# Two of four scans per unit take a constant start and carry the state in an extra column

## The chip, the cores and the metric

The kernel runs on one core of one Trainium2 chip. The metric is device microseconds of one execution. The kernel before takes 7170.91 us (median of 3 runs, 7170.88 to 7171.45). Its profile is of one further execution.

## The reference, cut to what matters

Two layers work on x of shape (4, 128, 128, 128), all in float32. The first is a Mamba block over L = 16384 positions per image with 256 inner channels and 16 states per channel, followed by a group norm, silu and a residual. The second layer mixes spectra of each channel with four filters (rfft2 and irfft2 as matrix products). The change touches only the recurrence of the first layer:

```python
def step(h, inp):
    d_t, B_t, C_t, u_t = inp
    dA = jnp.exp(d_t[:, :, None] * A)
    h = h * dA + d_t[:, :, None] * B_t[:, None, :] * u_t[:, :, None]
    y = jnp.einsum('bds,bs->bd', h, C_t)
    return (h, y)
```

`h` starts at zero for each image, and is carried over all 16384 positions.

## The kernel before, in words

`block0` is the first layer, `block1` the second. In `block0` time is cut into **chunks** of T = 512 positions, 32 to an image (`NCH`), 128 in all. Within a chunk the 256 channels times 16 states are 32 tiles of 128 partitions by 512 positions (32 channels by 4 states each). Four such tiles form a **unit**: half `j` of the channels (2), rotation `r` (4), so a chunk has 8 units, here u0 to u7 in order, and u6 is (j, r) = (1, 2). The four tiles of a unit are its **places** 0 to 3.

For each place the work is: ScalarE computes exp(delta*A) into a tile `da` (L393, "exp 0" to "exp 3" below); VectorE runs `tensor_tensor_scan` (L412, "scan 0" to "scan 3"), which computes state = da*state + du*B along the 512 positions, starting from the last state of the same tile of the chunk before (`last`, a [P, 2] tile `st`), or from the constant 0.0 where an image begins; the states are multiplied with C into `hb`; and TensorE sums `hb` over the states into `y` (L433). The products with C are GpSimd's for places 0 and 1 (L419, one instruction for both, the scans having written to an SBUF tile `h`) and VectorE's for places 2 and 3 (L414, the scans having written in place over `da`). `by_vector` (L347) makes exceptions: in odd chunks that are not "norming", place 1 of u6 is VectorE's too. In **norming** chunks (16 of 32 in each of the later three images, 48 of 128, in which the image before is normalised beside the scans) place 2 of u6 is GpSimd's.

du*B comes from two places. For places 1 to 3 GpSimd multiplies it into `hb` (L363). For place 0 TensorE turns it into PSUM (`dbu_turn`, L383, four transposes, "the turn", tile `b0`). `b0` and `da` of places 1, 2 and 3 are PSUM tiles of one bank each, with one buffer each; `da` of place 0 lies in SBUF with two buffers.

The order on every engine is written out by hand: each chunk has 16 slots, two per unit (even slot: places 0 and 1, odd slot: places 2 and 3), and each slot goes through the phases of L552 in order. Each engine's queue is what that walk emits. Dependencies between engines are semaphore waits that the tile framework inserts; PSUM accesses to one bank are ordered by bank. The parts that matter here:

- ScalarE, in the odd slot of unit u: exp 1 of unit u+1 (phase "exps"); the copy of the last states of places 0 and 1 (`st<-h`, phase "late", L420, shown as L554); the chunk's other work ("act", "pool"); exp 0 of unit u+2 ("early"); the two copies of the last states of places 2 and 3 (`st<-da`, L415). In the next even slot: exp 2 and exp 3 of unit u+1, then other work.
- TensorE, in the odd slot of unit u: the turn of unit u+1 first, then sums of unit u-1, then the chunk's other matmuls.
- GpSimd: `dbu` of unit u+1, then the product with C of unit u.

The other work of ScalarE for the next chunk sits in fixed slots (L323 to L332): silu and z in slot 2 (u1), softplus in slot 6 (u3), the turned copies `bt` in slots 8 to 14, of which those of slots 8 and 11 wait for transposes `pt_dut` of TensorE that precede them directly. From chunk 52 on, transforms of the second layer are mixed in (`spectrum`, slots 12 and 13, L468).

Of the kernel before, what the change touches and what calls it, by code (L numbers as in the profile page):

```python
# [26 lines left out]
F32 = mybir.dt.float32  # L27
AF = mybir.ActivationFunctionType
ALU = mybir.AluOpType
# [4 lines left out]
P = 128  # L34
T = 512
DG = 32
SQ = 4
NP = 16
# [8 lines left out]
def kernel(ctx: ExitStack, tc: tile.TileContext, a: dict, out: bass.AP):  # L47
# [101 lines left out]
    spec = [dpool.tile([H, C, 2, WF], F32, tag=f"spec_{b}", name=f"spec_{b}") for b in range(EARLY)]  # L149
    shared = SimpleNamespace(**{k: v for k, v in locals().items() if k not in ("ctx", "tc")})  # L150
    block0(tc, shared)
    block1(tc, shared)


def block0(tc, s):
    nc, B, NCH, NH, NS, NG, ND, R, NX, KC, HALO, C, L, NF, DI = (
        s.nc, s.B, s.NCH, s.NH, s.NS, s.NG, s.ND, s.R, s.NX, s.KC, s.HALO, s.C, s.L, s.NF, s.DI,
    )
    NT = T // P
    with ExitStack() as ctx:  # L160
        def pool(name, bufs, **kw):
            return ctx.enter_context(tc.tile_pool(name=name, bufs=bufs, **kw))

        p1 = pool("p1", 1)
        p2 = pool("p2", 2)
        hpool = pool("hb", 4)
        tiny = pool("tiny", 2)
# [5 lines left out]
        psd = pool("psd", 1, space=PSUM)  # L173
# [4 lines left out]
        def turn_bank(n):  # L178
            return pst.tile([P, T], F32, tag="pt", name=f"pt_{n}")

        st = {}
        stats, outs = s.stats, s.outs

# [154 lines left out]
        def norming(k):  # L338

            return k >= NCH and 2 <= k % NCH < 2 + NCH // 2  # L340

        def place(r, p):


            return (p - r) % ND

        def by_vector(k, j, r, p):  # L347

            if norming(k):
                return p > 1 and (j, r, p) != (1, 2, 2)  # L350
            return p > 1 or (k % 2 == 1 and (j, r, p) == (1, 2, 1))

        def dbu(u):

            k, r = divmod(u, NH * NG)
            j, r = divmod(r, NG)
            d = st[k]
            hb = d["hb", j, r] = hpool.tile([P, ND, T], F32, tag="hb", name=f"hb_{k}_{j}_{r}")
            p = 1
            while p < NG:  # L360
                m = place(r, p)
                n = min(NG - p, ND - m)
                nc.gpsimd.tensor_tensor(  # L363
                    hb[:, p : p + n, :], d["du", j][:, m : m + n, :], d["B"][:, p - 1 : p - 1 + n, :], ALU.mult
                )
                p += n

        def pair(n):

            k, r = divmod(n, NP)  # L370
            u, p = divmod(r, ND // 2)
            j, r = divmod(u, NG)
            return k, j, r, 2 * p

        def dbu_turn(n):

            k, j, r, p = pair(n)
            d = st[k]
            if p == 0:
                b = d["b0"] = psd.tile([P, T], F32, tag="b0", name=f"b0_{k}_{j}_{r}")  # L380
                for t in range(NT):
                    src = d["bt"][:, t, j * ND + place(r, 0), :, :].rearrange("p s d -> p (s d)")
                    nc.tensor.transpose(b[:, t * P : (t + 1) * P], src, s.ident)  # L383

        def exps(n, qs):

            k, j, r, p = pair(n)
            d = st[k]
            for q in qs:
                m = place(r, p + q)  # L390
                c = (j * NG + p + q) * ND + m
                da = (psd if p + q else p2).tile([P, T], F32, tag=f"da{p + q}", name=f"da{p + q}_{k}_{j}_{r}")
                nc.scalar.activation(da, d["delta", j][:, m, :], AF.Exp, scale=s.amat[:, c : c + 1])  # L393
                d["da", j, r, p + q] = da

        def scans(n):


            k, j, r, p = pair(n)
            d = st[k]  # L400
            hb = d["hb", j, r]
            das = [d.pop(("da", j, r, p + q)) for q in range(2)]
            dve = [q for q in range(2) if by_vector(k, j, r, p + q)]
            pool = [q for q in range(2) if q not in dve]
            last = d["last", j, r, p] = tiny.tile([P, 2], F32, tag=f"st{j}_{r}_{p}", name=f"st_{k}_{j}_{r}_{p}")
            if pool:
                h = p2.tile([P, 2, T], F32, tag="h", name=f"h_{k}_{j}_{r}_{p}", bufs=3)
            for q in range(2):
                b = hb[:, p + q, :] if p + q else d.pop("b0")
                init = 0.0 if k % NCH == 0 else st[k - 1]["last", j, r, p][:, q : q + 1]  # L410
                o = das[q] if q in dve else h[:, q, :]
                nc.vector.tensor_tensor_scan(o, das[q], b, init, ALU.mult, ALU.add)  # L412
            for q in dve:
                nc.vector.tensor_tensor(hb[:, p + q, :], das[q], d["C"][:, p + q, :], ALU.mult)  # L414
                nc.scalar.copy(last[:, q : q + 1], das[q][:, T - 1 : T])  # L415
            if pool:
                q = slice(pool[0], pool[-1] + 1)
                ps = slice(p + pool[0], p + pool[-1] + 1)
                nc.gpsimd.tensor_tensor(hb[:, ps, :], h[:, q, :], d["C"][:, ps, :], ALU.mult)  # L419
                todo[n + 1, "late"].append(partial(nc.scalar.copy, last[:, q], h[:, q, T - 1]))  # L420

        def sums(u):

            k, r = divmod(u, NH * NG)
            j, r = divmod(r, NG)
            d = st[k]
            if r == 0:
                y = d["y", j] = psy.tile([P, T], F32, tag="y", name=f"y_{k}_{j}")
                nc.tensor.matmul(y, s.diag[:, j, :], d["u"][:, j, :], start=True, stop=False)  # L429
            y = d["y", j]  # L430
            for p in range(ND):
                m = place(r, p)
                nc.tensor.matmul(  # L433
                    y[m * DG : (m + 1) * DG, :], s.sel, d["hb", j, r][:, p, :], start=False, stop=r == NG - 1
                )

        def post(k):
# [66 lines left out]
        n_chunks = B * NCH  # L504
        todo = defaultdict(list)
# [33 lines left out]
        for n in range(n_chunks * NP):  # L539
            if n % 2 == 0:  # L540
                todo[n - 3, "early"].append(partial(exps, n, (0,)))
            todo[n - 1, "exps"].append(partial(exps, n, (1,) if n % 2 == 0 else (0, 1)))
            todo[n - 1, "turn"].append(partial(dbu_turn, n))
            todo[n, "scans"].append(partial(scans, n))
            if n % 2 == 0:
                todo[n - 2, "dbu"].append(partial(dbu, n // 2))
            else:
                todo[n + 2, "sums"].append(partial(sums, n // 2))
        slots = [n for n, _ in todo]
        with tc.manual_schedule():  # L550
            for n in range(min(slots), max(slots) + 1):
                for phase in ("turn", "sums", "pe", "exps", "late", "act", "pool", "dbu", "early", "gate", "scans", "dve", "end"):  # L552
                    for f in todo[n, phase]:
                        f()  # L554

# [500 lines left out]
```

## Time and profile before

| what | value |
|---|---|
| median of 3 runs | 7170.91 us |
| the profiled execution | 7175.45 us, of which the span from first to last instruction is 7173.6 us |
| VectorE busy in the span | 6892.9 us (96%) |
| GpSimd busy | 6892.5 us (96%) |
| ScalarE busy | 6143.9 us (86%) |
| TensorE busy | 5904.2 us (82%), mean granted clock 0.897 |
| scans (L412) | 4096 of about 1.2 us |
| `block0` | from the start to about 6408 us; the rest is `block1` |

The busy shares are averages over stages. In `block0` a chunk takes 48.37 us (even) or 49.12 us (odd) where nothing else is mixed in, and 50.30 us where norming is. In the groups of instructions each row has a line, an engine, an operation, the tiles out<-in, and then busy time, mean nanoseconds of one and the idle time before it with what ended it. In the timeline each row has start, duration, engine, line and operation, and in brackets the engine's idle time before it and what ended it; on VectorE and ScalarE the next instruction starts some 0.08 us before the one before it ends, so what an instruction costs its engine is the distance of starts.

### The profile page before, as it was taken

What the parts mean: (1) busy time and instruction counts of PE and PEld (TensorE: products, weight loads), DVE (VectorE), ACT (ScalarE), POOL (GpSimd) and SP (SyncE); (2) the same over time, 40 slices, a digit from 0 to 9 for tenths busy, and PEclk for the clock granted to TensorE, in tenths of its full rate; (3) what the DMA queues carried; (4) which work ended last, traced back from release to release, by engine and by line L of the source; (5) the groups of instructions that cost most, each with busy time, mean ns of one, the idle gap of its engine ahead of it and who ended that gap; (6) DMA issues with size and microseconds to landing.
All of it is one profiled execution on the core that took longest, in us unless ns stands there. A gap on an engine that the chain in (4) does not pass through costs nothing.

```text
span 7173.6 us, 91384 instructions
## 1 busy us (share of the span) xinstructions
PE 5904.2 (82%) x26708; PEld 2626.8 (37%) x26708; DVE 6892.9 (96%) x7966; ACT 6143.9 (86%) x13658; POOL 6892.5 (96%) x3188
## 2 busy tenths in 40 slices
PE   6888888788787788888888788888887888867998
PEld 2333333233222233333333333333333333326888
DVE  6999999999999999999999999999999999989777
ACT  6888888888888888888888888898888888878876
POOL 6999999999999999999999999999999999988887
PEclk8888888888888889998989899999898899979999
DMA  5666666666777777777777777777777777769866
GB/s 139 160 160 152 163 159 151 165 159 165 191 176 192 179 171 176 172 184 175 189 196 186 188 176 175 178 177 184 189 191 194 177 179 177 172 164 306 236 185 162
DMA packets 905480, 1286.20 MB, mean 179 GB/s; under 512 B 81672, under 2 KB 356752, under 8 KB 904976
## 3 DMA queue, kind: packets, MB, share of 16 engines
q1 hardware_dynamic: 904832, 1280.09, 71.9%
q8 instruction: 210, 3.44, 0.2%
q14 instruction: 294, 2.41, 0.1%
q10 hardware_dynamic: 144, 0.26, 0.0%
HBM read 1023.45 MB, written 256.58 MB: 178 GB/s over the span
## 4 chain that ended last, share of the span: by engine, by line
DVE 41%; ACT 29%; issue 11%; PE 10%; DMA 5%; POOL 3%; SPq 1%; DVEq 0%; ACTq 0%; POOLq 0%
DVE da L412 20%; DVE h L412 12%; ACT da L393 12%; DVE hb L414 5%; ACT L393 3%; DMA rdelta<-dd 2%; ACT L275 2%; ACT delta L275 2%; ACT bt L304 2%; POOL hb L363 2%; DVE zs L443 1%; PE y L433 1%; POOL hb L419 1%; ACT L242 1%; DMA xt<-x 1%
## 5 line engine op out<-in xcount | busy, mean ns | idle before, releaser
L363 POOL TENSOR_TENSOR hb<-rdu,rB 128x1536 f32<-128x1536 f32 (+2 forms) x1536 | 3605.7, 2364 | 22.4 <-DMA rdelta<-dd 21.3
L393 ACT ACTIVATE da<-rdelta,amat 128x512 f32<-128x512 f32 x4096 | 2794.1, 700 | 138.3 <-DVE h L412 133.9
L419 POOL TENSOR_TENSOR hb<-h,rC 128x1024 f32<-128x1024 f32 (+1 forms) x1072 | 2435.0, 2274 | 88.8 <-DVE h L412 73.4
L412 DVE TENSOR_TENSOR_SCAN da<-da,st,hb 128x512 f32<-128x512 f32 x1976 | 2419.8, 1267 | 21.5 <-ACT da L393 14.3
L433 PE MATMUL y<-hb,sel 128*32 128x512 f32 x8192 | 1313.4, 717 | 2.9 <-POOL hb L419 2.7
L414 DVE TENSOR_TENSOR hb<-da,rC 128x512 f32<-128x512 f32 x2040 | 1296.1, 674 | 3.0
L412 DVE TENSOR_TENSOR_SCAN h<-da,st,b 128x512 f32<-128x512 f32 x992 | 1258.3, 1268 | 1.7 <-PE b L383 1.6
L412 DVE TENSOR_TENSOR_SCAN h<-da,st,hb 128x512 f32<-128x512 f32 x1000 | 1251.6, 1255 | 1.8 <-ACT da L393 1.8
L383 PE MATMUL b<-ident,bt 128*128 128x128 f32 x4096 | 748.4, 305 | 516.1 <-DVE h L412 390.6
L234 PE MATMUL pp_cv<-xm,wck 128*128 128x512 f32 x2048 | 1014.3, 640 | 1.6 <-ACT xm L217 0.8
L304 ACT ACTIVATE bt<-pt_dut,xdt 128x256 f32<-128x256 f32 x2048 | 839.4, 474 | 184.5 <-PE pt_dut L293 184.3
L383 PEld LDWEIGHTS b<-ident,bt 128*128 128x128 f32 x4096 | 531.3, 154 | 1017.1 <-DVE h L412 692.8
L415 ACT COPY st<-da 128x1 f32<-128x1 f32 x2040 | 273.1, 160 | 474.2 <-DVE hb L414 471.1
L234 PEld LDWEIGHTS pp_cv<-xm,wck 128*128 128x128 f32 x2048 | 395.9, 204 | 651.0 <-issue 422.1
L828 POOL TENSOR_TENSOR wb<-wb,term 128x1040 f32<-128x1040 f32 x192 | 461.0, 2401 | 70.8 <-ACT term L822 62.9
L293 PE MATMUL pt_dut<-ident,du 128*128 128x128 f32 x1024 | 232.4, 338 | 285.1 <-ACT xdt L286 174.9
L429 PE MATMUL y<-u,diag 128*128 128x512 f32 x512 | 303.0, 675 | 188.7 <-DVE zs L443 187.3
L293 PEld LDWEIGHTS pt_dut<-ident,du 128*128 128x128 f32 x1024 | 132.2, 162 | 604.8 <-POOL du L312 475.9
L393 ACT ACT_TABLE_LOAD x262 | 336.1, 1283 | 12.1 <-DMA rdelta<-dd 7.4
L312 POOL TENSOR_TENSOR du<-delta,u 128x512 f32<-128x512 f32 x256 | 318.8, 1267 | 25.8 <-ACT delta L275 25.8
L223 PE MATMUL pp_z<-xm,win 128*128 128x512 f32 x512 | 274.5, 634 | 51.8 <-ACT fq L497 46.2
L267 PE MATMUL pp_dt<-xd,wdt 8*128 8x512 f32 x512 | 284.8, 642 | 33.0 <-ACT pp_o L457 23.5
(160 smaller groups left out, 8139.8 us busy)
## 6 DMA issues: line engine op xcount, KB each, us to landing
rdelta<-dd SPq DMA_DIRECT2D x1024, 256.0 KB, 4.7
rdu<-dd SPq DMA_DIRECT2D x1024, 256.0 KB, 7.5
rC<-bc SPq DMA_DIRECT2D x512, 256.0 KB, 7.3
rB<-bc SPq DMA_DIRECT2D x512, 192.0 KB, 4.7
dd<-delta SPq DMA_DIRECT2D x256, 256.0 KB, 7.2
dd<-du SPq DMA_DIRECT2D x256, 256.0 KB, 5.7
ft<-in_filt_w SPq DMA_DIRECT2D x104, 520.0 KB, 7.0
ob<-o SPq DMA_DIRECT2D x128, 256.0 KB, 2.1
```

Source lines behind the costliest of these rows:

```text
L234: nc.tensor.matmul(ps["cv", j], w, d["xm"][:, t : t + T], start=t == 0, stop=t == KC - 1)
L293: nc.tensor.transpose(ps["dut"][:, 2 * t + j, :], d["du"][:, j, at : at + P], s.ident)
L304: nc.scalar.activation(d["bt"][:, 2 * h + t, :, q, :], src, AF.Copy, scale=d["xdt"][:, 2 * h + t, R + q : R + q + 1])
L312: nc.gpsimd.tensor_tensor(du, d["delta"][:, j, :], d["u"][:, j, :], ALU.mult)
L363: nc.gpsimd.tensor_tensor(hb[:, p : p + n, :], d["du", j][:, m : m + n, :], d["B"][:, p - 1 : p - 1 + n, :], ALU.mult)
L383: nc.tensor.transpose(b[:, t * P : (t + 1) * P], src, s.ident)
L393: nc.scalar.activation(da, d["delta", j][:, m, :], AF.Exp, scale=s.amat[:, c : c + 1])
L412: nc.vector.tensor_tensor_scan(o, das[q], b, init, ALU.mult, ALU.add)
L414: nc.vector.tensor_tensor(hb[:, p + q, :], das[q], d["C"][:, p + q, :], ALU.mult)
L419: nc.gpsimd.tensor_tensor(hb[:, ps, :], h[:, q, :], d["C"][:, ps, :], ALU.mult)
L433: nc.tensor.matmul(y[m * DG : (m + 1) * DG, :], s.sel, d["hb", j, r][:, p, :], start=False, stop=r == NG - 1)
L828: nc.gpsimd.tensor_tensor(wb, wb, u[n].terms[f], ALU.add)
```

## The change

The scans of places 1 and 2 become 513 columns long and start from the constant 0.0. Their first column holds the last state of the chunk before: `hb` gets one more column in front (`1 + T`), into which a new small ScalarE copy (`carry`, phase "carry" in the odd slot before the unit, after "late") writes the two states; at an image's start GpSimd clears it instead. The first column's factor does not matter, since it multiplies the constant 0.0: it is whatever lies in PSUM just before `da`. For that, `b0` and `da` of places 1 and 2 become one tile `band` of three banks, and the scan of place 1 reads from the last column of `b0` on, that of place 2 from the last column of `da` of place 1 on. The scan of place 2 also writes that column when it runs in place.

Since the scan of place 2 now touches the bank of place 1, exp 1 of the next unit is issued after the scans of the odd slot, no longer at the slot's start. `last` becomes one [P, 4] tile per unit. `by_vector` gives place 1 of u6 to VectorE in even chunks too (outside norming ones); that unit (in which the scans of places 1 and 2 keep their pointer to the state) is the one that `carried` leaves out.

```diff
--- before.py
+++ after.py
@@ -178,6 +178,7 @@
         def turn_bank(n):
             return pst.tile([P, T], F32, tag="pt", name=f"pt_{n}")
 
+        band = psd.tile([P, 3 * T], F32, tag="band", name="band")
         st = {}
         stats, outs = s.stats, s.outs
 
@@ -348,22 +349,37 @@
 
             if norming(k):
                 return p > 1 and (j, r, p) != (1, 2, 2)
-            return p > 1 or (k % 2 == 1 and (j, r, p) == (1, 2, 1))
+            return p > 1 or (j, r, p) == (1, 2, 1)
 
         def dbu(u):
 
             k, r = divmod(u, NH * NG)
             j, r = divmod(r, NG)
             d = st[k]
-            hb = d["hb", j, r] = hpool.tile([P, ND, T], F32, tag="hb", name=f"hb_{k}_{j}_{r}")
+            hb = d["hb", j, r] = hpool.tile([P, ND, 1 + T], F32, tag="hb", name=f"hb_{k}_{j}_{r}")
             p = 1
             while p < NG:
                 m = place(r, p)
                 n = min(NG - p, ND - m)
                 nc.gpsimd.tensor_tensor(
-                    hb[:, p : p + n, :], d["du", j][:, m : m + n, :], d["B"][:, p - 1 : p - 1 + n, :], ALU.mult
+                    hb[:, p : p + n, 1:], d["du", j][:, m : m + n, :], d["B"][:, p - 1 : p - 1 + n, :], ALU.mult
                 )
                 p += n
+
+        def carried(k, j, r):
+
+            return () if by_vector(k, j, r, 1) else (1, 2)
+
+        def carry(u):
+
+            k, r = divmod(u, NH * NG)
+            j, r = divmod(r, NG)
+            if carried(k, j, r):
+                o = st[k]["hb", j, r][:, 1:3, 0]
+                if k % NCH == 0:
+                    nc.gpsimd.memset(o, 0.0)
+                else:
+                    nc.scalar.copy(o, st[k - 1]["last", j, r][:, 1:3])
 
         def pair(n):
 
@@ -377,7 +393,7 @@
             k, j, r, p = pair(n)
             d = st[k]
             if p == 0:
-                b = d["b0"] = psd.tile([P, T], F32, tag="b0", name=f"b0_{k}_{j}_{r}")
+                b = band[:, 0:T]
                 for t in range(NT):
                     src = d["bt"][:, t, j * ND + place(r, 0), :, :].rearrange("p s d -> p (s d)")
                     nc.tensor.transpose(b[:, t * P : (t + 1) * P], src, s.ident)
@@ -389,7 +405,10 @@
             for q in qs:
                 m = place(r, p + q)
                 c = (j * NG + p + q) * ND + m
-                da = (psd if p + q else p2).tile([P, T], F32, tag=f"da{p + q}", name=f"da{p + q}_{k}_{j}_{r}")
+                if p + q in (1, 2):
+                    da = band[:, (p + q) * T : (p + q + 1) * T]
+                else:
+                    da = (psd if p else p2).tile([P, T], F32, tag=f"da{p + q}", name=f"da{p + q}_{k}_{j}_{r}")
                 nc.scalar.activation(da, d["delta", j][:, m, :], AF.Exp, scale=s.amat[:, c : c + 1])
                 d["da", j, r, p + q] = da
 
@@ -402,22 +421,31 @@
             das = [d.pop(("da", j, r, p + q)) for q in range(2)]
             dve = [q for q in range(2) if by_vector(k, j, r, p + q)]
             pool = [q for q in range(2) if q not in dve]
-            last = d["last", j, r, p] = tiny.tile([P, 2], F32, tag=f"st{j}_{r}_{p}", name=f"st_{k}_{j}_{r}_{p}")
+            if p == 0:
+                d["last", j, r] = tiny.tile([P, ND], F32, tag=f"st{j}_{r}", name=f"st_{k}_{j}_{r}")
+            last = d["last", j, r][:, p : p + 2]
             if pool:
-                h = p2.tile([P, 2, T], F32, tag="h", name=f"h_{k}_{j}_{r}_{p}", bufs=3)
+                h = p2.tile([P, 2, 1 + T], F32, tag="h", name=f"h_{k}_{j}_{r}_{p}", bufs=3)
             for q in range(2):
-                b = hb[:, p + q, :] if p + q else d.pop("b0")
-                init = 0.0 if k % NCH == 0 else st[k - 1]["last", j, r, p][:, q : q + 1]
-                o = das[q] if q in dve else h[:, q, :]
+                if p + q in carried(k, j, r):
+                    a = band[:, (p + q) * T - 1 : (p + q + 1) * T]
+                    o = a if q in dve else h[:, q, :]
+                    nc.vector.tensor_tensor_scan(o, a, hb[:, p + q, :], 0.0, ALU.mult, ALU.add)
+                    continue
+                b = hb[:, p + q, 1:] if p + q else band[:, 0:T]
+                init = 0.0 if k % NCH == 0 else st[k - 1]["last", j, r][:, p + q : p + q + 1]
+                o = das[q] if q in dve else h[:, q, 1:]
                 nc.vector.tensor_tensor_scan(o, das[q], b, init, ALU.mult, ALU.add)
+            if p and n + 1 < n_chunks * NP:
+                exps(n + 1, (1,))
             for q in dve:
-                nc.vector.tensor_tensor(hb[:, p + q, :], das[q], d["C"][:, p + q, :], ALU.mult)
+                nc.vector.tensor_tensor(hb[:, p + q, 1:], das[q], d["C"][:, p + q, :], ALU.mult)
                 nc.scalar.copy(last[:, q : q + 1], das[q][:, T - 1 : T])
             if pool:
                 q = slice(pool[0], pool[-1] + 1)
                 ps = slice(p + pool[0], p + pool[-1] + 1)
-                nc.gpsimd.tensor_tensor(hb[:, ps, :], h[:, q, :], d["C"][:, ps, :], ALU.mult)
-                todo[n + 1, "late"].append(partial(nc.scalar.copy, last[:, q], h[:, q, T - 1]))
+                nc.gpsimd.tensor_tensor(hb[:, ps, 1:], h[:, q, 1:], d["C"][:, ps, :], ALU.mult)
+                todo[n + 1, "late"].append(partial(nc.scalar.copy, last[:, q], h[:, q, T]))
 
         def sums(u):
 
@@ -431,7 +459,7 @@
             for p in range(ND):
                 m = place(r, p)
                 nc.tensor.matmul(
-                    y[m * DG : (m + 1) * DG, :], s.sel, d["hb", j, r][:, p, :], start=False, stop=r == NG - 1
+                    y[m * DG : (m + 1) * DG, :], s.sel, d["hb", j, r][:, p, 1:], start=False, stop=r == NG - 1
                 )
 
         def post(k):
@@ -539,17 +567,19 @@
         for n in range(n_chunks * NP):
             if n % 2 == 0:
                 todo[n - 3, "early"].append(partial(exps, n, (0,)))
-            todo[n - 1, "exps"].append(partial(exps, n, (1,) if n % 2 == 0 else (0, 1)))
+            if n % 2 or n == 0:
+                todo[n - 1, "exps"].append(partial(exps, n, (0, 1) if n % 2 else (1,)))
             todo[n - 1, "turn"].append(partial(dbu_turn, n))
             todo[n, "scans"].append(partial(scans, n))
             if n % 2 == 0:
                 todo[n - 2, "dbu"].append(partial(dbu, n // 2))
+                todo[n - 1, "carry"].append(partial(carry, n // 2))
             else:
                 todo[n + 2, "sums"].append(partial(sums, n // 2))
         slots = [n for n, _ in todo]
         with tc.manual_schedule():
             for n in range(min(slots), max(slots) + 1):
-                for phase in ("turn", "sums", "pe", "exps", "late", "act", "pool", "dbu", "early", "gate", "scans", "dve", "end"):
+                for phase in ("turn", "sums", "pe", "exps", "late", "carry", "act", "pool", "dbu", "early", "gate", "scans", "dve", "end"):
                     for f in todo[n, phase]:
                         f()
 
```

## The prediction

> **What bounds the kernel now.** I read the page first. VectorE and GpSimd are both at 96%, and the mean hides stages, so I went on to the table of windows (columns: window, length, then busy of PE, PEld, DVE, ACT, POOL, clock, DMA):
>
> ```profile
> 200.00:1600.00 1400.00, 1150.30 (x4379) 427.55 (x4382) 1399.52 (x1453) 1201.23 (x2682) 1387.90 (x632) 0.86 0.66 157
> 1900.00:2400.00 500.00, 401.93 (x1514) 146.09 (x1514) 499.66 (x527) 430.38 (x946) 497.79 (x230) 0.87 0.74 184
> ```
>
> VectorE never pauses: it is the bound, in plain chunks (first row) as in norming ones (second). The waits of GpSimd say how close behind it is: in the first window it waits 8.3 us for VectorE's scans (0.29 us a chunk of 48.6), in the second 1.6 us in ten chunks. So in norming chunks only 0.16 us a chunk can be gained before GpSimd bounds.
>
> ScalarE is at 86%, but not evenly. The timeline of chunk 10 around u1 and u2, first ScalarE, then VectorE:
>
> ```profile
> 561.75 0.16 ACT L415 COPY st<-da 128x1 f32<-128x1 f32 x1 [0.44 <-DVE hb L414]
> 561.80 1.31 ACT L393 ACTIVATE da<-rdelta,amat 128x512 f32<-128x512 f32 x2
> ...
> 566.65 1.28 ACT L393 ACT_TABLE_LOAD   x1
> 567.94 0.69 ACT L393 ACTIVATE da<-rdelta,amat 128x512 f32<-128x512 f32 x1
> 568.57 0.18 ACT L554 COPY st<-h 128x2 f32<-128x2 f32 x1
> 568.65 0.72 ACT L393 ACTIVATE da<-rdelta,amat 128x512 f32<-128x512 f32 x1
> 569.28 0.20 ACT L415 COPY st<-da 128x1 f32<-128x1 f32 x2
> ```
>
> ```profile
> 568.12 1.27 DVE L412 TENSOR_TENSOR_SCAN h<-da,st,b 128x512 f32<-128x512 f32 x1
> 569.31 1.25 DVE L412 TENSOR_TENSOR_SCAN h<-da,st,hb 128x512 f32<-128x512 f32 x1
> ```
>
> At 561.75 ScalarE is released by VectorE's last product of u0, and then works without a gap. At 567.94 stands exp 1 of u2, at 568.65 exp 0 of u3; scan 1 of u2 starts at 569.31, 0.68 us after its input is ready. That is the cover that the change spends.
>
> **Part 1, the constant start.** The groups by shape show both kinds of scan, since images begin with a constant: `h<-da,st,hb` 1255 ns against `h<-da,hb` 1195, `da<-da,st,hb` 1267 against 1209. The distances of starts agree (1.175 against 1.115 us). So 60 ns less; the 513th column costs 1195/512 = 2 ns (at most). Net 58 ns. Units with carried scans: 7 of 8 in 80 plain chunks, 8 of 8 in 48 norming ones; the four chunks that begin an image gain nothing.
> - Plain: 76 x 14 x 0.058 = 61.7 us off VectorE's path.
> - Norming: 48 x 16 x 0.058 = 44.5 us off VectorE, of which GpSimd lets 48 x 0.16 = 7.7 us through. GpSimd's own work there is unchanged.
> - Not shown: a scan operand over two PSUM banks. Nearest rows: 1255 ns (`da` in PSUM, b in SBUF) and 1268 (the reverse), so -13 to +13 ns each, up to 14 us either way over the plain chunks' 1064 scans; I take 0, the row's own shape. Rows of 513 columns no longer join into one run: GpSimd's 520 elements in runs of 65 cost 1298 ns, against 1276 for 512 contiguous plus 8 x 2.12 = 1293. Nothing.
>
> **Part 2, place 1 of u6 in 40 even plain chunks.** GpSimd loses half of a product (2363 to 1276 ns, 43 us in all, not on the path). VectorE gains a product: in chunk 10 (even) u6 to u7 is 5.90 us, in odd ones 6.64, as the product also waits for its own scan to drain. 40 x 0.74 = **+29.6 us**.
>
> **Part 3, the new copy.** Some 916 on ScalarE. Like `st<-h` it lasts 0.18 us but moves the next start by 0.08 (568.57 to 568.65): 0.09 each, 0.6 us a chunk, where ScalarE idles 14% (6.8 us). It costs where ScalarE runs without a gap, so it goes into part 4. The 28 clears on GpSimd (about 0.1 us, MEMSET row) are nothing.
>
> **Part 4, exp 1 moves behind exp 0 of the next unit** and behind all other work of its slot, and waits for scan 2 besides. Scan 2 ends 3.5 us before scan 1 of the next unit starts, so this wait alone costs nothing. The queue does. Its place after the change: start of exp 0 of the unit after (moved up by 0.62 us unless a wait stands between; down by 0.09 for the copy), plus 0.62 for exp 0, plus 0.70 for itself, plus 0.05 for the hand-over. For u2 of chunk 10: 568.65 - 0.62 + 0.09 + 0.62 + 0.70 + 0.05 = 569.49, against 569.31: 0.17 late (unrounded). I counted this through the timeline for every unit:
> - u2, plain: 0.17 late in 78 chunks. Released by u0's end, so the saving in u1 (0.12) is lost too: 78 x 0.29 = **22.6 us**.
> - u4 (softplus in front): 0.01 late, and u3's saving lost: 80 x 0.13 = **10.4 us**.
> - u5, from chunk 50 on: 46 x 0.10 = **4.6 us**.
> - u6: exp 1 now stands behind the turned copy `bt` of slot 11, which waits for TensorE's `pt_dut`. In the first image that leaves 0.12 us to spare. Later not always; chunk 59, ScalarE, VectorE, then TensorE:
>
> ```profile
> 3008.53 0.71 ACT L393 ACTIVATE da<-rdelta,amat 128x512 f32<-128x512 f32 x1
> 3009.14 0.21 ACT L554 COPY st<-h 128x2 f32<-128x2 f32 x1
> 3011.39 0.47 ACT L304 ACTIVATE bt<-pt_dut,xdt 128x256 f32<-128x256 f32 x1 [2.04 <-PE pt_dut L293]
> 3011.76 0.71 ACT L393 ACTIVATE da<-rdelta,amat 128x512 f32<-128x512 f32 x1
> ```
>
> ```profile
> 3011.61 1.26 DVE L412 TENSOR_TENSOR_SCAN da<-da,st,hb 128x512 f32<-128x512 f32 x1
> ```
>
> ```profile
> 3005.25 0.66 PE L383 MATMUL b<-ident,bt 128*128 128x128 f32 x4 [1.71 <-DVE h L412]
> 3007.00 2.05 PE L429 MATMUL y<-u,diag 128*128 128x512 f32 x2 [1.09 <-DVE zs L443]
> 3008.98 1.78 PE L433 MATMUL y<-hb,sel 128*32 128x512 f32 x8
> ```
>
> Exp 1 of u6 (today at 3008.53) would start at 3011.76 + 0.62 = 3012.38 and be ready at 3013.13, while scan 1 starts at 3011.61: 1.5 us late. Such are 29 chunks, nearly all after chunk 50, 40.1 us together, and 0.06 of saving lost in each: **41.8 us**. The cause is TensorE's clock: 0.74 granted from 3004 to 3010.5 against 0.93 in chunk 10 (586 to 593), and y takes 2.05 us instead of 1.12.
> - u0 in 11 chunks with an aggregation in slot 15 (`pt_agg`, for which ScalarE waits): **10 us**. u7 in 6 chunks behind a group norm's root: **14 us**.
>
> **Part 5, the turn** now waits for scan 1, 1.18 us later than scan 0. Behind it on TensorE stand sums and the chunk's matmuls. In chunk 10 the turn starts after scan 1's end or within 0.5 us of it in five of eight units; for u4, u7 and u0 TensorE idles afterwards (3.5 and 2.3 us before the next work, or a wait for `bt`). Its readers (scan 0, y's first matmul behind the gate) have over 0.05 us: 0, at worst the 0.5 us of lateness before u6 in 46 chunks, 23 us.
>
> The row bears a rule: the clock fell after TensorE had worked 0.66 us in the 3.5 us before 3007. The Trainium skill ("TensorE: Matmul & The Clock Gate", Part 1) says that the clock halves after an idle window of about 3.4 us; the trace halves it with 0.66 us of work inside. By the rule taken strictly no further chunk falls, and the u6 term stays. By the row, more of the 46 chunks could fall, at 1.5 us each, 26 us at most. The stretch's ends (pp_h before, y behind the gate after) do not move with the turn, so I keep 29.
>
> **Sum.** -61.7 - 7.7 + 29.6 + 22.6 + 10.4 + 4.6 + 41.8 + 10 + 14 = +63.6 us. Against the profiled execution: 7175.45 + 64 = 7239. The median of the runs stands 4.5 us below that execution: 7170.91 + 64 = **7235 us**, 0.9% slower.
>
> **Rivals.**
> 1. *The cover holds* (faster). If exp 1 is in time everywhere, only VectorE's terms remain: -61.7 - 7.7 + 29.6 = -40, **7131 us**. For it: ScalarE idles 14%, and work that moves up before exp 1 can release TensorE earlier. Against: 0.68 us of cover at u2 against 0.70 + 0.09 put before it. It decides if exp 1 of u2 and u6 ends by scan 1's start.
> 2. *Only u6 is relieved* (about no change): the transposes come early enough, so 41.8, 10 and half of 14 us fall away: +5, **7176 us**.
> 3. *TensorE's lateness spreads* (part 5's 23 us, 17 more cold chunks at 1.5, 26 us): +113, **7284 us**. For: `pt_dut` and `bt` waits of 184 us already. Against: the ends that do not move.
>
> **How the numbers follow.** Forecast 0.55 (its own range 7200 to 7270), rival 1 0.22, rival 2 0.10, rival 3 0.13. Bounds of the unknown: banks 14 us, the copy at 0.18 instead of 0.09 in 158 late units 14 us, cold chunks -42 to +26. The range 7130 to 7300 takes in all but the outer parts of rivals 1 and 3. What a measurement of this kernel tells from no change is about 0.2% (14 us): faster 0.23, same 0.10, slower 0.67.
>
> **What will show it.** Right: scans of places 1 and 2 at about 1.20 us; VectorE idle before L412, ended by ScalarE's exp, of some 100 us where today it is 16; chunk periods of about 48.7 us in the first image, odd and even (today 49.12 and 48.37), 50.14 in norming. Wrong: that idle stays near 16 us (rival 1), scans over two banks at 1.25 us or more, GpSimd's products longer, or VectorE waiting for the turn or for `hb`.

## The result and the profile after

| | before | after |
|---|---|---|
| median | 7171.18 us (4 runs beside the ones after) | 9722.58 us (4 runs, 9713.51 to 9730.90) |
| ratio | 1 | 1.3557, 95% interval 1.3533 to 1.3580 |
| the profiled execution | 7175.45 us | 9730.9 us, of which the span is 9729.1 |
| mean granted TensorE clock | 0.897 | 0.814 |
| a unit, mean of all (from the starts of scan 0) | 6.21 us | 8.71 us |

The forecast was 7235 us, the range 7130 to 7300. Slower was right, but the size was off by a factor of forty: what the forecast counted makes up a small part of the loss, and no rival named the rest.

The page of the kernel after, its busy line:

```profile
PE 6653.4 (68%) x26708; PEld 2864.6 (29%) x26708; DVE 7055.8 (73%) x8006; ACT 6404.6 (66%) x14614; POOL 6714.5 (69%) x3216
```

VectorE's busy time rose by 163 us only (6892.9 before). It is 73% of a longer span: the time went into idling, on all engines at once. The table of windows of the kernel after, the same two windows as in the prediction (PE, PEld, DVE, ACT, POOL, clock, DMA):

```profile
200.00:1600.00 1400.00, 933.72 (x3130) 329.41 (x3122) 1030.73 (x1046) 898.98 (x2068) 959.62 (x452) 0.79 0.48 113
1900.00:2400.00 500.00, 338.81 (x1116) 119.39 (x1112) 366.76 (x377) 321.93 (x739) 339.03 (x166) 0.78 0.49 115
```

VectorE was at 1399.52 of 1400 before, and is at 1030.73 now. No engine is at 80%, so the engines wait for each other, and the view to read next is the waits. VectorE's waits in the kernel after (us in total, times, longest):

```profile
DVE h L438 <- ACT band L412: 917.3, 975, 43.4
DVE band L433 <- PE band L399: 754.3, 893, 2.0
DVE hb L442 <- ACT band L412: 586.2, 270, 3.9
...
DVE band L438 <- PE band L399: 70.1, 45, 1.8
DVE h L433 <- PE band L399: 65.0, 48, 1.9
DVE band L438 <- ACT bt L305: 54.6, 35, 1.8
```

L438 and L433 are the scans (pointer and constant start), L442 VectorE's product with C, L412 the exponentials, L399 the turn. The three large rows are, in order: scan 0 waits for an exponential; scan 2 waits for the turn; the product of place 2 waits for an exponential. Together the six rows are 2447 us (43 of them a single wait at the start of the kernel). One unit shows which exponential and which turn. The timeline of VectorE, then TensorE, then ScalarE, kernel after:

```profile
1016.02 1.28 DVE L438 TENSOR_TENSOR_SCAN h<-da,st,band 128x512 f32<-128x512 f32 x1 [0.82 <-ACT band L412]
1017.22 1.20 DVE L433 TENSOR_TENSOR_SCAN h<-band,hb 128x513 f32<-128x513 f32 x1
1019.26 1.23 DVE L433 TENSOR_TENSOR_SCAN band<-band,hb 128x513 f32<-128x513 f32 x1 [0.84 <-PE band L399]
1020.41 1.27 DVE L438 TENSOR_TENSOR_SCAN da<-da,st,hb 128x512 f32<-128x512 f32 x1
1021.58 0.67 DVE L442 TENSOR_TENSOR hb<-band,rC 128x512 f32<-128x512 f32 x1
1022.17 0.68 DVE L442 TENSOR_TENSOR hb<-da,rC 128x512 f32<-128x512 f32 x1
1023.67 1.28 DVE L438 TENSOR_TENSOR_SCAN h<-da,st,band 128x512 f32<-128x512 f32 x1 [0.82 <-ACT band L412]
```

```profile
1018.57 0.66 PE L399 MATMUL band<-ident,bt 128*128 128x128 f32 x4 [2.18 <-DVE h L433]
```

```profile
1020.53 0.69 ACT L412 ACTIVATE band<-rdelta,amat 128x512 f32<-128x512 f32 x1 [0.20 <-DVE band L433]
1022.29 0.16 ACT L443 COPY st<-band 128x1 f32<-128x1 f32 x1 [1.06 <-DVE hb L442]
1022.88 0.16 ACT L443 COPY st<-da 128x1 f32<-128x1 f32 x1 [0.43 <-DVE hb L442]
1022.94 0.70 ACT L412 ACTIVATE band<-rdelta,amat 128x512 f32<-128x512 f32 x1
```

Scan 1 ends at 1018.42. The turn of the next unit starts 0.15 us after that and ends at 1019.23; scan 2 starts 0.03 us later. Scan 2 ends at 1020.49, exp 1 starts 0.04 us later. Exp 2, the last ScalarE row, is queued behind the copies of the last states, as it was before; it ends at 1023.64 and scan 0 starts 0.03 us later. So within each unit the accesses to `band` run one after the other: scan 0, scan 1, turn, scan 2, exp 1, product of place 2, exp 2, and again. Three pairs of these neighbours share no column and no bank: the turn (bank 0) and scan 2 (banks 1 and 2); exp 1 (bank 1) and the product of place 2 (bank 2); exp 2 (bank 2) and scan 0 (bank 0). Two reads are put in order too: the copy `st<-band` only reads `band`, as the product before it does, and starts 0.04 us after that product's end (1022.25), though scan 2 had written the state by 1020.49. The kernel before does the same within one bank: its copies `st<-da` that ScalarE idled for start 0.03 us after a product's end (median of 810). The unit takes 7.65 us (1016.02 to 1023.67), of which 1.66 us are the two gaps.

The theory to test, **W**: accesses of different engines to one PSUM tile are put in the order of the program, **whatever bank** they touch. The rival, **B**: they are ordered by bank, as the section on the kernel before says and the prediction took for granted, and something else makes the gaps (the 513-column scans over two banks, the moved exponential).

### The profile page after: what moved, and what is told of

It reads as the page before. It is cut to its first block, busy times and chain, and to the rows that moved or that the text cites. A ratio compares the mean times of both kernels' runs of the same rounds, so it can differ in the third digit from the quotient of the medians.

```text
span 9729.1 us, 93128 instructions
## 1 busy us (share of the span) xinstructions
PE 6653.4 (68%) x26708; PEld 2864.6 (29%) x26708; DVE 7055.8 (73%) x8006; ACT 6404.6 (66%) x14614; POOL 6714.5 (69%) x3216
## 4 chain that ended last, share of the span: by engine, by line
DVE 39%; ACT 28%; PE 15%; DMA 8%; issue 6%; SPq 3%; POOL 0%; DVEq 0%; ACTq 0%; POOLq 0%
DVE hb L442 12%; DVE h L438 8%; ACT band L412 8%; DVE da L438 6%; DVE h L433 6%; PE band L399 5%; ACT da L412 4%; DMA rdu<-dd 4%; DVE band L433 3%; PE y L461 3%; ACT L412 3%; DMA xt<-in_x 2%; SPq L321 2%; PE y L457 2%; DVE band L438 2%
## 5 line engine op out<-in xcount | busy, mean ns | idle before, releaser
L399 PE MATMUL band<-ident,bt 128*128 128x128 f32 x4096 | 873.1, 352 | 2653.0 <-DVE h L433 2192.1
L438 DVE TENSOR_TENSOR_SCAN h<-da,st,band 128x512 f32<-128x512 f32 x992 | 1270.1, 1280 | 848.3 <-ACT band L412 847.0
L433 DVE TENSOR_TENSOR_SCAN band<-band,hb 128x513 f32<-128x513 f32 x896 | 1104.8, 1233 | 754.4 <-PE band L399 754.3
L412 ACT ACTIVATE band<-rdelta,amat 128x512 f32<-128x512 f32 x2048 | 1416.0, 691 | 334.6 <-DVE band L433 256.0
L399 PEld LDWEIGHTS band<-ident,bt 128*128 128x128 f32 x4096 | 574.9, 177 | 3305.5 <-issue 1679.8
L412 ACT ACTIVATE da<-rdelta,amat 128x512 f32<-128x512 f32 x2048 | 1438.3, 702 | 3.1
L438 DVE TENSOR_TENSOR_SCAN da<-da,st,hb 128x512 f32<-128x512 f32 x992 | 1256.3, 1266 | 0.0
L433 DVE TENSOR_TENSOR_SCAN h<-band,hb 128x513 f32<-128x513 f32 x992 | 1191.0, 1201 | 65.6 <-PE band L399 65.0
L442 DVE TENSOR_TENSOR hb<-band,rC 128x512 f32<-128x512 f32 x1056 | 719.9, 682 | 600.5 <-ACT band L412 586.2
L442 DVE TENSOR_TENSOR hb<-da,rC 128x512 f32<-128x512 f32 x1024 | 695.4, 679 | 1.6
```

The costliest lines, as they stand in the source:

```text
L433: nc.vector.tensor_tensor_scan(o, a, hb[:, p + q, :], 0.0, ALU.mult, ALU.add)
L442: nc.vector.tensor_tensor(hb[:, p + q, 1:], das[q], d["C"][:, p + q, :], ALU.mult)
```

## The experiments

**e1: the kernel before with one tile for three banks, and nothing else.**

```diff
+        band = psd.tile([P, 3 * T], F32, tag="band", name="band")
...
-                b = d["b0"] = psd.tile([P, T], F32, tag="b0", name=f"b0_{k}_{j}_{r}")
+                b = d["b0"] = band[:, 0:T]
...
-                da = (psd if p + q else p2).tile([P, T], F32, tag=f"da{p + q}", name=f"da{p + q}_{k}_{j}_{r}")
+                if p + q in (1, 2):
+                    da = band[:, (p + q) * T : (p + q + 1) * T]
+                else:
+                    da = (psd if p else p2).tile([P, T], F32, tag=f"da{p + q}", name=f"da{p + q}_{k}_{j}_{r}")
```

> The kernel before with one edit: the turned du*B and the exponentials of places 1 and 2 lie in one PSUM tile of three banks; scans, starts and order stay as they were, and no access reaches over a bank's border. Theory W (accesses to one PSUM tile wait for each other in program order whatever the bank): scan 2 then waits for the turn and for exp 1 of the next unit, scan 0 for exp 2; with the stalls that the changed kernel shows (0.84 us for the turn, 0.82 for exp 2) and 0.8 more for exp 1 in the same gap a unit takes 8.4 us or more instead of 5.9, 9300 to 10500 us in all. Theory B (ordered by bank; the scans over the border tie the banks together): nothing changes, 7171 us within 0.2%.

Measured: **10484.6 us** (one run), 3314 us over the kernel before (7170.58). The page counts the same instructions on every engine as before (7966 on VectorE, 13658 on ScalarE), no scan has 513 columns, no exponential is moved. The groups of e1 by shape (busy us, mean ns, then idle before and what ended it):

```profile
L416 DVE TENSOR_TENSOR_SCAN band<-band,st,hb 128x512 f32<-128x512 f32 x984 | 1271.1, 1292 | 2065.6 <-ACT band L397 2059.1 <-ACT st L558 2.3
L416 DVE TENSOR_TENSOR_SCAN h<-da,st,band 128x512 f32<-128x512 f32 x992 | 1269.1, 1279 | 908.4 <-ACT band L397 908.4
L416 DVE TENSOR_TENSOR_SCAN h<-band,st,hb 128x512 f32<-128x512 f32 x1000 | 1259.2, 1259 | 79.6 <-ACT band L397 79.6
```

The scans themselves last 1259 to 1292 ns, against 1255 to 1268 before. Scan 2 (first row) waits 2059 us for an exponential, and in the old order that is exp 1 of the next unit, issued ahead of it and writing another bank. One case in e1, TensorE's turn, ScalarE's exp 1 and VectorE's scan 2:

```profile
999.20 0.63 PE L384 MATMUL band<-ident,bt 128*128 128x128 f32 x4 [3.79 <-DVE h L416]
```

```profile
999.91 0.69 ACT L397 ACTIVATE band<-rdelta,amat 128x512 f32<-128x512 f32 x1 [0.46 <-PE band L384]
```

```profile
1000.64 1.29 DVE L416 TENSOR_TENSOR_SCAN band<-band,st,hb 128x512 f32<-128x512 f32 x1 [1.00 <-ACT band L397]
```

The turn (bank 0) ends at 999.83, exp 1 (bank 1) starts 0.08 us after it and ends at 1000.60, scan 2 (bank 2) starts 0.04 us after that. Shown: the tile alone does it, W holds and B falls; the time lies at the upper end of W's range. The edit also makes the tile once, where the three were made anew for each unit. No run tells these two apart, but the waits join accesses that have nothing but the tile in common. The old order of exponentials is even worse for a shared tile than the new one (10485 against 9723), since exp 1 then stands between scan 1 and scan 2.

**e2 to e4: the change without the tile, then undone part by part.** In e2, `b0` and `da` of places 1 and 2 have tiles of their own again; these scans take 512 columns from the constant 0.0, and the carry copy is still made, but the carried state of places 1 and 2 is left out of the result. e3 is e2 with exp 1 at its old place. e4 is e3 with the old share of u6.

```diff
-                    a = band[:, (p + q) * T - 1 : (p + q + 1) * T]
-                    o = a if q in dve else h[:, q, :]
-                    nc.vector.tensor_tensor_scan(o, a, hb[:, p + q, :], 0.0, ALU.mult, ALU.add)
+                    o = das[q] if q in dve else h[:, q, 1:]
+                    nc.vector.tensor_tensor_scan(o, das[q], hb[:, p + q, 1:], 0.0, ALU.mult, ALU.add)
```

```diff
-            if p and n + 1 < n_chunks * NP:
-                exps(n + 1, (1,))
...
-            if n % 2 or n == 0:
-                todo[n - 1, "exps"].append(partial(exps, n, (0, 1) if n % 2 else (1,)))
+            todo[n - 1, "exps"].append(partial(exps, n, (1,) if n % 2 == 0 else (0, 1)))
```

```diff
-            return p > 1 or (j, r, p) == (1, 2, 1)
+            return p > 1 or (k % 2 == 1 and (j, r, p) == (1, 2, 1))
```

> The changed kernel with the one tile taken apart again into three tiles, so its scans of places 1 and 2 are 512 columns from the constant 0.0; the small copy into hb, the later exp 1 and place 1 of u6 on VectorE stay. Left out: the carried state of places 1 and 2 (each chunk starts them at zero). Theories W and B both: the large loss goes. What is left tests the prediction's other steps: 7235 us less the saving of two columns if exp 1 is late as counted (u2, u4, u6 and so on, 103 us); about 7131 if it is in time everywhere; over 7300 if the order of exp 1 (theory O) is what costs.

> As the run with three tiles, and exp 1 of the next unit issued at the odd slot's start as in the kernel before. Left out: the carried state of places 1 and 2. All theories: exp 1 in time, so VectorE's terms alone remain: -61.7 - 7.7 + 29.6, about 7131 us, up to 14 us more if the small copies delay ScalarE where it has no gap. The difference to the run with the late exp 1 is the price of the order: 103 us by the count.

> As the run with exp 1 in its old place, and place 1 of u6 in even chunks GpSimd's again. Left out: the carried state of places 1 and 2. VectorE's terms alone would give 7171 - 62 - 8 = 7101, but GpSimd waited only 0.29 us a plain chunk and 0.16 a norming one, so it becomes the bound: 80 x 0.29 + 8 = 31 us gained, 7140. If GpSimd has more room than its waits show: 7101.

| kernel | us (median) | ratio to before, interval | chunk, first image, even / odd | norming chunk, second image |
|---|---|---|---|---|
| before (same chip) | 7170.58 | 1 | 48.37 / 49.12 | 50.30 |
| e2: tiles apart | 7211.90 | 1.0057 (1.0040 to 1.0074) | 48.83 / 48.82 | 49.53 |
| e3: old order too | 7094.06 | 0.9894 (0.9879 to 0.9909) | 48.32 / 48.32 | 49.33 |
| e4: old share too | 7064.25 | 0.9851 (0.9837 to 0.9866) | 47.44 / 48.32 | 49.33 |

So the four parts have prices. The tile: 9722.6 - 7211.9 = **+2510.7 us** (its 513th columns among it), beside 2447 us of waits in the kernel after. The late exp 1: 7211.9 - 7094.1 = **+117.8**. The share of u6: 7094.1 - 7064.3 = **+29.8**. The constant start with its copy and the rows of 513 columns: 7064.3 - 7170.6 = **-106.3**. The last two prices are not quite clean: with the old share, u6 of the even chunks starts its places 1 and 2 from a constant as well, 38 x 2 x 0.058 = 4.4 us by count, so the share alone costs 25 us by the times, 29 by the chunks (38 x 0.76). e3 lies 37 us below what was expected (7131), e4 37 us below the lower of its two numbers (7101). The norming chunks show why: they lose 0.97 us each where 0.16 was counted.

VectorE's waits in e2, the rows that the prediction named as its sign:

```profile
DVE da L433 <- ACT st L438: 57.4, 35, 3.0
DVE h L428 <- ACT st L438: 46.1, 110, 4.0
```

Scan 1 waits 103.5 us in 145 cases, where ScalarE comes late. The rows name ScalarE's copy that ended last before the scan; in 142 of the cases exp 1 had ended 0.10 us before it. The first row is u6, with its pointer start, the second the other units.

**e6: two banks in one tile.** In the changed kernel, `b0` gets its own bank back. Place 1 starts by pointer again, place 2 keeps its 513 columns.

```diff
-        band = psd.tile([P, 3 * T], F32, tag="band", name="band")
+        band = psd.tile([P, 2 * T], F32, tag="band", name="band")
...
-            return () if by_vector(k, j, r, 1) else (1, 2)
+            return () if by_vector(k, j, r, 1) else (2,)
...
-                b = band[:, 0:T]
+                b = d["b0"] = psd.tile([P, T], F32, tag="b0", name=f"b0_{k}_{j}_{r}")
```

> The changed kernel, but the tile `band` holds two banks (places 1 and 2); the turned du*B has its own bank again, so place 1 starts from the last state by pointer as before and place 2 takes 513 columns. The whole computation is done. Theory W (all accesses to one tile are put in order, whatever the bank): scan 2 no longer waits for the turn (754 + 70 us gone) and scan 0 no longer for exp 2 (917 us gone); what can stay is the product of place 2 behind exp 1 (586 us), so 7,300 to 8,000 us. Rival M (a tile of more than one bank, or a scan over a bank's border, costs as such): 9,000 us or more, with scan 2 longer than 1.25 us or waits at the same places.

Measured: **8621.64 us** (2 runs), ratio 1.2021 (1.1997 to 1.2045): between the ranges of the two theories. VectorE's large waits that remain in e6, and its two groups of scan 2 and the product:

```profile
DVE hb L442 <- ACT band L412: 1247.4, 773, 5.8
...
DVE h L438 <- ACT band L412: 14.9, 11, 4.7
```

```profile
L433 DVE TENSOR_TENSOR_SCAN band<-band,hb 128x513 f32<-128x513 f32 x896 | 1102.9, 1231 | 31.6
L442 DVE TENSOR_TENSOR hb<-band,rC 128x512 f32<-128x512 f32 x1056 | 727.9, 689 | 1253.1 <-ACT band L412 1247.4
```

The two waits that W said would go are gone (754 to 32 us, 917 to 15), and the scan over a bank's border lasts 1.23 us, so rival M falls. The wait that W let stay, the product of place 2 (bank 2) behind exp 1 (bank 1), doubled from 586 to 1247 us. W's number missed; presumably the gaps before the scans had given ScalarE time to catch up, and without them it is late more often (773 waits in place of 270). One such case in e6, VectorE and ScalarE:

```profile
1012.35 0.69 DVE L442 TENSOR_TENSOR hb<-band,rC 128x512 f32<-128x512 f32 x1 [2.46 <-ACT band L412]
```

```profile
1009.73 1.28 ACT L412 ACT_TABLE_LOAD   x1
1011.02 0.72 ACT L412 ACTIVATE da<-rdelta,amat 128x512 f32<-128x512 f32 x1
1011.65 0.67 ACT L412 ACTIVATE band<-rdelta,amat 128x512 f32<-128x512 f32 x1
```

ScalarE runs without a gap through other work and exp 0, and VectorE, which needs nothing of exp 1 here, stands until it has ended at 1012.32. A kernel that issues exp 1 behind that product as well was not run.

**r1 to r3: what made GpSimd quicker.** In e2 to e4 and in the kernel after, GpSimd's product with C of 1024 elements takes 2.19 us instead of 2.36, though nobody changed its work. What differs is the layout: rows of `h` and `hb` 513 columns apart, used from their second column on. r1 is the kernel before with both, r2 with `h` alone, r3 with `hb` alone. In r1 and r3 the last states of a unit also lie in one tile of four.

```diff
-                h = p2.tile([P, 2, T], F32, tag="h", name=f"h_{k}_{j}_{r}_{p}", bufs=3)
+                h = p2.tile([P, 2, 1 + T], F32, tag="h", name=f"h_{k}_{j}_{r}_{p}", bufs=3)
...
-                o = das[q] if q in dve else h[:, q, :]
+                o = das[q] if q in dve else h[:, q, 1:]
```

> The kernel before, with the rows of `h` and `hb` 513 columns apart and starting one column in, as in the changed kernel (the last states of a unit in one tile of four, for room); scans, exponentials and shares as before, column 0 is never used. Theory R (the row distance of 513 makes GpSimd's 128x1024 product with C quicker): 2.19 us for it instead of 2.36, and a time of 7,140 to 7,171, since VectorE bounds nearly everywhere. Rival S (what made it quicker is the scans' constant start or another part of the change): 2.36 us and 7,171 us.

> As the run with both, but only the rows of `h` (the product's input) are 513 columns apart. If the input's layout makes the product quick: 2.19 us; if the output's: 2.36 us. Time 7,140 to 7,171.

> As the run with both, but only the rows of `hb` (the product's output, and the output of du*B) are 513 columns apart. If the output's layout makes the product quick: 2.19 us, though du*B's 128x1024, with the same output, took 2.37 us in all kernels so far; if the input's: 2.36 us. Time 7,140 to 7,171.

GpSimd's groups, r2 and then r3:

```profile
L419 POOL TENSOR_TENSOR hb<-h,rC 128x1024 f32<-128x1024 f32 x984 | 2152.2, 2187 | 258.6 <-DVE h L412 255.1 <-DVE total L694 1.7 <-DMA spec<-fq 0.5
```

```profile
L421 POOL TENSOR_TENSOR hb<-h,rC 128x1024 f32<-128x1024 f32 x984 | 2325.1, 2363 | 84.3 <-DVE h L414 69.6 <-DVE total L696 1.4 <-DMA spec<-fq 1.3
L363 POOL TENSOR_TENSOR hb<-rdu,rB 128x1024 f32<-128x1024 f32 x512 | 1211.8, 2367 | 0.0
```

It is the input: 2187 ns with `h`'s rows apart, 2363 with `hb`'s. 984 x 0.176 = 173 us less GpSimd work, and no gain by itself: r1 takes 7181.84 (ratio 1.0012, 1.0003 to 1.0022), r2 7181.91 (1.0012), r3 7172.67 (1.0000), so r1 and r2 lie 11 us above the expected range. The chunks of the first image and the norming ones keep their lengths to 0.01 us in all three (medians), which says that VectorE bounds the norming chunks of the kernel before too. The +0.1% of r1 and r2 arises in the plain chunks beside the second layer, from the 50th on (mean 49.08 us before, 49.26 and 49.28 in r1 and r2); why is open.

**c3 and c5: carry the state without the shared tile.** These do the whole computation. Tiles are apart, exp 1 stays at its old place, and a one-column ScalarE instruction adds exp * last state into the first column of du*B.

```diff
+                    o = d["hb", j, r][:, p + q, 1:2]
+                    last = st[k - 1]["last", j, r][:, p + q : p + q + 1]
+                    nc.scalar.activation(o, d["da", j, r, p + q][:, 0:1], AF.Identity, scale=last, bias=o)
```

> The whole computation, every place in its own bank. Rows of 513 as in r1, and place 3 alone starts from a constant: a one-column ScalarE instruction adds exp * last state into the first column of du*B (992 of them, about 0.19 us each as the other short copies). By count 992 x 58 ns = 58 us less VectorE work: 7,182 - 58 = 7,124. Rival: ScalarE, 24 short instructions a chunk more than it had room for, is late: 7,130 to 7,200.

> As with place 3 alone, but places 1 and 3 start from a constant (1,984 short ScalarE instructions, some 3 us a chunk). By count 1,984 x 58 ns = 115 us less: 7,182 - 115 = 7,067. Rival: ScalarE (44 of 48.4 us a chunk, 47 with these) is late with exponentials, as it was in e2 for 118 us: 7,100 to 7,250.

> Places 1 and 3 as before, but the rows of `h` and `hb` lie 512 columns apart, as in the kernel before, so GpSimd's product with C should take 2.36 us again. If GpSimd then bounds, it lets only its own slack through (0.29 us in some 80 plain chunks, 0.16 in 48 norming ones: about 31 us): 7,172 - 31 = 7,141, and with quicker rows 74 us less. If the rows don't matter: the same as with them.

> Places 1, 2 and 3 start from a constant (2,976 short ScalarE instructions, some 4.5 us a chunk). By count 173 us less than 7,182: 7,009. Rival: ScalarE, at 88 % before it, has no room for 565 us more, and the fold for place 2 stands between exp 2 and scan 2: 7,100 to 7,300, with VectorE waiting before scan 2.

| constant start in | us | ratio, interval |
|---|---|---|
| place 3 (c3) | 7182.56 | 1.0015 (1.0006 to 1.0024) |
| places 1 and 3 (c3) | 7283.04 | 1.0154 (1.0139 to 1.0169) |
| places 1 and 3, rows contiguous (c5) | 7306.29 | 1.0183 (1.0167 to 1.0198) |
| places 1, 2, 3 (c3) | 7451.82 | 1.0388 (1.0371 to 1.0406) |

No gain in any; with one place the rival's range held the time, with two or three the time lies above even that, and c5 fits neither 7141 nor "the same". The group of the new instruction (places 1 and 3), and VectorE's waits there:

```profile
L405 ACT ACTIVATE hb<-da,hb,st 128x1 f32<-128x1 f32 x1984 | 697.4, 351 | 109.5 <-POOL hb L364 47.8 <-ACT st L568 2.6 <-ACT da L394 0.4
```

```profile
DVE da L425 <- ACT da L394: 103.9, 232, 3.5
DVE h L425 <- ACT hb L405: 74.0, 192, 1.5
```

The expectations priced it like the short copies, 0.19 us. It lasts 0.351, and the next ScalarE instruction starts 0.25 us after it (median), against 0.08 after the copy `st<-h` of the kernel before: 16 x 0.25 = 4 us a chunk. VectorE's scans save 0.9 us a chunk, and wait for ScalarE instead. The Trainium skill ("ScalarE: Activation LUTs", section "What ACT_TABLE_LOAD costs") gives 186 ns and 0.83 per column with immediate scale and bias, about 93 more for each [128,1] pointer operand, and 93 of overlap between neighbours; for one column and two pointers an estimate from that is 373 ns, 280 from start to start. The trace shows 351 and 250: nearer to this than to the copy's row (167 ns in the same run), which has no pointer.

c3 against c5 is the row distance, besides the last states' tile of four (which cost nothing in r3): 7283 against 7306. Over all 80 plain chunks both take 50.6 us on the mean, over the 48 norming ones 50.52 against 51.01, and 48 x 0.49 = 23.5 us is the whole difference. So where VectorE has less to do, GpSimd's speed counts in norming chunks.

## Why the prediction was wrong, point by point

- **What bounds now**: that VectorE bounds was right (r1: a quicker GpSimd shortens neither the chunks of the first image nor the norming ones). The mean plain chunk of that window is 48.75 us by the starts of scan 0, not 48.6; the 0.29 us stay.
- **Part 5, the turn, at 0** and **Part 4's "this wait alone costs nothing"**: these steps failed. Both priced only the waits that share a bank (the turn behind scan 1, exp 1 behind scan 2); no run measures those two alone. Part 5 names scan 0 and y's first matmul as the turn's readers, and so left out who else stands behind it. Three waits were put at nothing because they were not seen: scan 2 waits for that turn, the product of place 2 for that exp 1, scan 0 for exp 2 (754, 586 and 917 us in the kernel after). All three rest on the tile, not the bank. The premise stands in the section on the kernel before ("PSUM accesses to one bank are ordered by bank"). The trace of before couldn't refute it, since each of these tiles was one bank there, and by tile and by bank were the same. The prediction never asked it. e1 shows 3314 us from the tile alone, e2 the 2510.7 us that it costs in this order.
- The Trainium skill ("PSUM — Partial Sum Buffer", section "PSUM bank collisions raise a hardware error") says to guard PSUM by bank and quarter of the partitions, not by address. The waits here are wider than that rule. By the rule the three steps need no wait, and the time would be about e2's 7212; the runs show 9723. Whether the same kernel runs undisturbed without those waits wasn't tried.
- **Part 1, plain chunks, -61.7**: right. Even chunks lose 0.93 us (16 x 0.058), odd ones 0.79 (14 x 0.058 = 0.81), from before to e4; in the change both kinds have 14.
- **Part 1, norming, -44.5 of which 7.7 come through**: mis-sized. 50.30 to 49.33 us, so 48 x 0.97 = 47 us came through. "GpSimd's own work there is unchanged" was the wrong step: eight products a chunk, each 0.172 us shorter, are 1.4 us. By these numbers GpSimd was busy 497.79 of 500 before, 50.1 us of 50.30, and would have held the chunk above that; with 1.4 less it holds it at 48.7 only. e4 with contiguous rows was not run; c3 against c5 shows 0.49 us a norming chunk from the rows. The "Nothing" behind the rows of 513 had looked for a loss alone.
- **Scans over two banks, 0 within 14 us**: right. In the kernel after:

```profile
L433 DVE TENSOR_TENSOR_SCAN h<-band,hb 128x513 f32<-128x513 f32 x992 | 1191.0, 1201 | 65.6 <-PE band L399 65.0 <-POOL hb L380 0.6
L433 DVE TENSOR_TENSOR_SCAN band<-band,hb 128x513 f32<-128x513 f32 x896 | 1104.8, 1233 | 754.4 <-PE band L399 754.3
```

  e2's scans from a constant in one bank take 1207 and 1212 ns: -6 and +21 ns each, 992 x -0.006 + 896 x 0.021 = +13 us. The 21 ns come with the tile and not with the border: e1's 32 in-place scans from a constant, 512 columns inside one bank of `band`, take 1229 ns, and its 32 into `h` 1198.
- **Part 2, +29.6**: right. From e3 to e4 an even chunk of the first image loses 0.88 us (48.32 to 47.44); 2 x 0.058 of that are the constant starts of u6 that only e4 has, which leaves 0.76, where 0.74 was predicted. That the times differ by 29.8, so close to 29.6, is in part luck.
- **Part 3 and Part 4's queue, +103**: close, 117.8 (e3 to e2), with 103.5 us of waits at the place named. The sum is better than its terms. From the starts of scan 0, e2 less e3: u2 21.0 us (22.6 predicted), u4 28.2 (10.4; as much lies in norming chunks, for which nothing was counted), u5 8.7 (4.6), u6 56.8 (41.8), u0 and u7 together 4.2 (24).
- **Sum**: without the tile, -106.3 + 29.8 + 117.8 = +41.3, where the prediction had +63.6. The forecast described e2 (7212) and not the change.
- **The range**: VectorE waiting for the turn stood among the signs of being wrong, and the turn's price was 23 us at worst. It was priced by when the turn starts, not by who waits behind it.

## What to carry to other kernels

Before tiles of different engines are joined into one, list every pair of accesses by different engines to the joined tile in program order, and price each as a wait, whatever the addresses: 1024 units with three such pairs cost 2.45 us each here, for a saving of 0.12 us. If the trace has only one-bank tiles, it can't say how a larger one is ordered; a kernel that changes the tile and nothing else answers that in one run. And a small instruction is priced by a row with the same operands: pointers made a one-column instruction cost three times a copy's start distance.

## What the runs showed of the hardware that was not expected

- GpSimd's product of two times 512 elements takes 2187 ns when the rows of one input lie 513 columns apart and start at its second column (r2), and 2363 when they are contiguous (r3); the output's row distance has no effect, and the 512-element product is the same in both (1276 and 1278 ns). Why is open.
- A scan of 513 columns over the border of two PSUM banks takes 1201 ns (into `h`) or 1233 (in place), within 4 ns of one of 512 columns inside a bank of the same tile (1198 and 1229, e1).
- A one-column ScalarE instruction with scale and bias by pointer takes 351 ns, a plain copy of one column 167 (both in the run with places 1 and 3).
